# Two 3x3 convolutions on one Trainium2 core: four output columns from six terms in place of two from four

## The chip, the cores and the metric

The kernel runs on one core of one Trainium2 chip. The metric is the device time of one execution in microseconds (us), from the first to the last instruction and what lies around them; a kernel is run several times and the median is given. Engines are named as in the profile: PE is TensorE's matmul, PEld its weight load, DVE is VectorE, ACT is ScalarE, POOL is GpSimd, SP is SyncE, which here only issues transfers (DMA).

## The reference

x has 16 images of 128 channels and 32 x 32 points, all in float32. Two layers follow each other, each with a mixing part and a token part, both added to x. Layer 0 has a linear attention and a spectral filter bank (a long convolution over the 1024 tokens). Layer 1, which the change is about, is cut here to what matters:

```python
# mixing part: y = _ln_c(x), normalized over the channels
out = relu(_bn(_conv3x3(y, w1), gamma1, beta1, mean1, var1))
out = _bn(_conv3x3(out, w2), gamma2, beta2, mean2, var2)
x = x + relu(out + y)
# token part: t = _ln_t(x); 64 experts, each takes 8 tokens of an image
logits = einsum('bsd,ed->bse', t, gate_w) + gate_b
probs = softmax(logits, axis=1)                  # over the tokens
topv, topi = top_k(probs, 8)                     # by expert
# gather, weigh and sum the tokens, two linear maps with gelu, scatter back
```

The convolutions have 128 input and 128 output channels, a 3 x 3 window and a border of zeros.

## The kernel before

The program has four stretches. **Layer 0, attention** goes over the 16 samples in a period that is written out by hand (`period`): one pass issues steps of several samples, one after the other. Between them, `prepare()` prepares layer 1's weights on POOL, one step for each pass: it loads a convolution's weights (`raw`), scales them by the batch norm's factor, makes the transformed taps in `pcw`, and stores them to DRAM (`cwd`). Then it loads and scales the table of an inverse transform (`pwi`, stored as `wid`). POOL also makes the butterflies of that layer's spectra. **Layer 0, filters** (`generate` and `multiply`) follows, and ends when the spectra `ys` are stored to `yd`.

**Layer 1** is one class, `Routed`, whose methods are the steps of one sample. A function, `planned`, decides the order in which all steps of all 16 samples are issued: it takes a table that names, for each step, its engine, an assumed duration, a due time, the steps it depends on and the buffers it opens and closes, and lists the steps by a simulated start. Each engine then works through its own steps in that order, so an instruction that waits holds up everything behind it on its engine. For each sample the steps are:

- `even`, `odd`, `odd_turn`, `odd_out`, `inverse`, `add`: the inverse transform of layer 0's spectrum (L958 to L1048); PE's part is L1039, 32 instructions of 128 columns.
- `tokens` to `norm`: transposes to tokens (L149), statistics on DVE (L132), scales on POOL (L996 to L1001), normalization on ACT (L141).
- `image`, `image_copy`: transposes back (L159) and an ACT copy (L1083) into `pads`, where the image lies as two planes, of odd and of even columns, each with a border of zeros.
- The first convolution: `terms` (four DVE subtractions and additions of column planes, L920), products (L926) in two halves of the image, 16 rows each: `middle` and `outer` take two terms each. `shift` (L1097, ACT) moves the first product of `middle` out of PSUM with the batch norm's shift, `sums` (L1105, L1106) and `rows` (L1115, L1116) combine the products on DVE into the even and odd columns, and `relu` (L1119, ACT) writes them into a third pair of planes.
- The second convolution, in the same way, where `rows2` also adds the image and then relu and x (L1143, L1145).
- `tokens2` to `channels_copy`: the same normalization for the token part (copy L1158, transposes L159, copy L1179).
- For each pair of samples: logits (L1187), the choice of eight tokens (L1199 to L1220 on DVE, L1212 on ACT), and the pooled tokens (L1242, L1253).

The convolution uses the minimal scheme for two columns and three taps: four terms of four neighbouring columns, one product each with transformed taps, and two columns out of their sums. The three rows of taps (`dy`) are summed in PSUM. One product is a matmul of 128 channels by 128 channels over 256 columns, and each float32 matmul is two instructions in the profile. So one convolution of a sample has 4 terms x 3 `dy` x 2 halves = 24 matmuls, 48 instructions.

PSUM holds three sorts of tiles here: `big` (two buffers of 1024 columns), `cv` (three of 512, for the products) and `s`. In SBUF, `v` (the terms), `r` and `cs` have two buffers each.

**The experts** (`hidden`, `turn`, `output`, `collect`) go over 16 groups of four experts. Their weights are 32 blocks of 1 MB (`we`), and nine are loaded ahead into buffers that layer 1 no longer needs (`RING` names them): five once the last sample's inverse is done, four after its last `rows2`. Each further block waits until its buffer's block is used. At the end the outputs are scattered with one matmul per half (L1461), added to x and stored.

Of the kernel before, what the change touches and what calls it, by code (L numbers as in the profile page):

```python
# [57 lines left out]
HP = H + 2  # L58
WP = W // 2 + 1
HR = H // 2  # L60
WT = W // 2
# [5 lines left out]
def metaformer_kernel(ctx: ExitStack, tc: tile.TileContext, io: dict, out: bass.AP):  # L67
# [96 lines left out]
    with ExitStack() as l0:  # L164
# [7 lines left out]
        cwd = [dram.tile([P, 3, 4, C], F32, name=f"cwd{n}", tag=f"cwd{n}") for n in range(2)]  # L172
# [35 lines left out]
        with ExitStack() as a0:  # L208
# [462 lines left out]
            def prepare():  # L671
# [4 lines left out]
                for n in range(2):  # L676
                    raw = ppool.tile([P, 3, 3, C], F32, name="raw", tag="raw")
                    nc.sync.dma_start(raw.rearrange("p a b c -> p (a b) c"), io[f"w{n + 1}"])
                    cw = ppool.tile([P, 3, 4, C], F32, name="pcw", tag="pcw")
                    yield  # L680
                    scale = srow[:, n, :].unsqueeze(1).to_broadcast([P, 3, C])
                    for k in range(3):
                        eng.tensor_tensor(raw[:, :, k], raw[:, :, k], scale, ALU.mult)
                        yield
                    eng.tensor_tensor(cw[:, :, 1], raw[:, :, 0], raw[:, :, 2], ALU.add)
                    yield
                    eng.tensor_tensor(cw[:, :, 2], cw[:, :, 1], raw[:, :, 1], ALU.subtract)
                    yield
                    eng.tensor_tensor(cw[:, :, 1], cw[:, :, 1], raw[:, :, 1], ALU.add)
                    yield  # L690
                    for k, r in ((0, 0), (3, 2)):
                        nc.sync.dma_start(cwd[n][:, :, k], raw[:, :, r])
                    eng.tensor_scalar(cw[:, :, 1:3], cw[:, :, 1:3], 0.5, None, ALU.mult)
                    nc.sync.dma_start(cwd[n][:, :, 1:3], cw[:, :, 1:3])
                    yield
# [34 lines left out]
            with tc.manual_schedule(engines=PINNED):  # L730
                for p in range(-reach, B):
                    next(preparing, None)
# [117 lines left out]
    b1 = gpool.tile([E, HID], F32, name="b1")  # L850
# [4 lines left out]
    with ExitStack() as c1:  # L855
# [10 lines left out]
        RING = ("y", "z", "zt", "wi", "y", "v", "v", "cw", "pad")  # L866
        FIRST = ("wi", "v", "cw", "pad", "y")
# [23 lines left out]
        cws = first.tile([P, 2, 3, 4, C], F32, name="cw", tag="cw")  # L891
        cw = [cws[:, n] for n in range(2)]
# [8 lines left out]
        nc.sync.dma_start(b1, w1[:, C, :])  # L901


        pads = first.tile([P, 3, 2, HP, WP], F32, name="pads", tag="pad")
        nc.gpsimd.memset(pads, 0.0)

        def inner(t, hf=None):

            r0, nr = (1, H) if hf is None else (1 + hf * HR, HR)
            return bass.AP(  # L910
                t.tensor, t.offset + r0 * WP, [t.ap[0], [HP * WP + 1, 2], [WP, nr], [1, WT]]
            )

        def terms(v, p, ks):

            d = [p[:, 1 - i % 2, :, i // 2 : i // 2 + WT] for i in range(4)]
            for k in ks:
                i, j, op = ((0, 2, ALU.subtract), (1, 2, ALU.add),
                            (2, 1, ALU.subtract), (1, 3, ALU.subtract))[k]
                nc.vector.tensor_tensor(v[:, k], d[i], d[j], op)  # L920

        def products(v, wt, hf, ks):
            pc = ps.tile([P, 2, HR, WT], F32, name="pcv", tag="cv", bufs=3)
            for i, k in enumerate(ks):
                for dy in range(3):
                    nc.tensor.matmul(  # L926
                        pc[:, i], wt[:, dy, k, :], v[:, k, hf * HR + dy : hf * HR + dy + HR],
                        start=(dy == 0), stop=(dy == 2),
# [77 lines left out]
        class Routed:  # L1006


            def __init__(self, b):
                self.b = b  # L1010
                self.pr, self.j = divmod(b, 2)
                self.p1, self.p2 = pads[:, b % 2], pads[:, 2]
                self.x = xt[b]
                self.y = yts[b].rearrange("p r x e -> p (r x) e")
                self.pm, self.po, self.sd, self.r, self.ct = {}, {}, {}, {}, {}
# [66 lines left out]
            def image_copy(self):  # L1082
                nc.scalar.copy(inner(self.p1), self.px.rearrange("p (h w o) -> p o h w", w=WT, o=2))  # L1083

            def term_tile(self):
                self.v = first.tile([P, 4, HP, WT], F32, name="v", tag="v", bufs=2)

            def terms(self):
                self.term_tile()
                terms(self.v, self.p1, (1, 2, 0, 3))  # L1090

            def middle(self, hf, n=0):
                self.pm[hf] = products(self.v, cw[n], hf, (1, 2))

            def shift(self, hf, n=0):
                self.ct[hf] = work.tile([P, HR, WT], F32, name="ct", tag="ct")
                nc.scalar.activation(  # L1097
                    self.ct[hf], self.pm[hf][:, 0], AF.Identity, bias=bn[:, n, 1:2]
                )

            def sums(self, hf):

                sd = self.sd[hf] = work.tile([P, 2, HR, WT], F32, name="cs", tag="cs")
                t, pc = self.ct[hf], self.pm[hf]
                nc.vector.tensor_tensor(sd[:, 0], pc[:, 1], t, ALU.add)  # L1105
                nc.vector.scalar_tensor_tensor(sd[:, 1], pc[:, 1], -1.0, t, ALU.mult, ALU.add)  # L1106

            def outer(self, hf, n=0):
                self.po[hf] = products(self.v, cw[n], hf, (0, 3))

            def rows(self, hf):

                r = self.r[hf] = work.tile([P, 2, HR, WT], F32, name="r", tag="r")
                sd, pc = self.sd[hf], self.po[hf]
                nc.vector.tensor_tensor(r[:, 0], pc[:, 0], sd[:, 0], ALU.add)  # L1115
                nc.vector.scalar_tensor_tensor(r[:, 1], pc[:, 1], -1.0, sd[:, 1], ALU.mult, ALU.add)  # L1116

            def relu(self, hf):
                nc.scalar.activation(inner(self.p2, hf), self.r[hf], AF.Relu)  # L1119

            def terms_middle(self):
                self.term_tile()
                terms(self.v, self.p2, (1, 2))

            def terms_outer(self):
                terms(self.v, self.p2, (0, 3))

            def middle2(self, hf):
                self.middle(hf, 1)

            def shift2(self, hf):
                self.shift(hf, 1)

            def sums2(self, hf):
                self.sums(hf)

            def outer2(self, hf):
                self.outer(hf, 1)

            def rows2(self, hf):  # L1140
                self.rows(hf)
                r = self.r[hf]
                nc.vector.tensor_tensor(r, r, inner(self.p1, hf), ALU.add)  # L1143
                xh = self.x[:, hf * HALF : (hf + 1) * HALF].rearrange("p (n o) -> p o n", o=2)
                nc.vector.scalar_tensor_tensor(  # L1145
                    xh, r.rearrange("p o h w -> p o (h w)"), 0.0, xh, ALU.max, ALU.add
# [117 lines left out]
            ("even", "POOL", 1.85, -409.2, "", "z", ""),  # L1264
            ("odd", "DVE", 1.4, 60, "", "zt", ""),
            ("odd_turn", "DVE", 0.75, -162.8, "odd", "", ""),
            ("odd_out", "DVE", 1.4, 308, "odd_turn even", "", "zt"),
            ("inverse", "PE", 3.5, -181.4, "even odd_out", "big:0", "z"),
            ("add", "DVE", 1.25, 32, "inverse", "", "big:0"),
            ("tokens", "PE", 0.88, -255.4, "add", "big:1", ""),  # L1270
            ("stats", "DVE", 1.4, 65, "tokens", "", "big:1"),
            ("copy", "ACT", 1.02, -202.6, "tokens", "tok", "big:1"),
            ("variance", "POOL", 0.22, -174.5, "stats", "", ""),
            ("root", "ACT", 0.52, -164.6, "stats", "", ""),
            ("scales", "POOL", 1.75, -338.7, "variance root", "", ""),
            ("norm 0", "ACT", 0.8, -46.1, "scales copy", "", ""),
            ("norm 1", "ACT", 2.35, -0.2, "norm0", "", ""),
            ("image", "PE", 0.88, -200.9, "norm1", "big:2", "tok"),
            ("image_copy", "ACT", 1.02, -154.9, "image", "p1", "big:2"),
            ("terms", "DVE", 2.6, -242.7, "image_copy", "v:0", ""),  # L1280
            ("middle 0", "PE", 2.6, -433, "terms", "cv:0m", "v:0"),
            ("shift 0", "ACT", 0.48, -171, "middle0", "", ""),
            ("sums 0", "DVE", 0.74, -165.9, "shift0", "cs:0", "cv:0m"),
            ("outer 0", "PE", 2.6, -360.9, "terms", "cv:0o", "v:0"),
            ("rows 0", "DVE", 0.74, -387.6, "outer0 sums0", "r:0", "cv:0o cs:0"),
            ("relu 0", "ACT", 0.64, -76.6, "rows0", "p2", "r:0"),
            ("middle 1", "PE", 2.6, -189.2, "terms middle0", "cv:1m", "v:0"),
            ("shift 1", "ACT", 0.48, 17.7, "middle1", "", ""),
            ("sums 1", "DVE", 0.74, -262.2, "shift1", "cs:1", "cv:1m"),
# [311 lines left out]
```

## Time and profile before

| | us |
|---|---|
| median of three runs | 1324.69 (1323.67 to 1330.67) |
| profiled execution | 1324.0 |
| its span, first to last instruction | 1322.2 |
| layer 0, attention | 0 to 396 |
| layer 0, filters | 396 to 695 |
| layer 1: fill, run, drain | 695 to 724, 724 to 1187, 1187 to 1217 |
| experts, output | 1217 to 1293, 1293 to 1322 |

The times of the stretches count from the span's start. The mean granted clock of TensorE is 0.971 of full speed. In the profile, "L926" is line 926 of the program; a group of instructions is shown with what it writes and reads, its shape, its count, its busy time and mean duration, and the idle time of its engine just before it with what ended that. The chain of waits goes back from the last instruction to whatever released each step. An engine that is busy all the time need not be the limit, and idle time of an engine that nothing waits for costs nothing.

### The profile page before, as it was taken

How to read it: one execution, taken by the hardware profiler on the slowest of the kernel's cores; microseconds unless marked ns; L12 is line 12 of the kernel's file. 1: busy time of each engine (PE TensorE's matmuls, PEld its weight loads, DVE VectorE, ACT ScalarE, POOL GpSimd, SP SyncE). 2: the span in 40 equal slices, each digit the busy share in tenths (PEclk: the TensorE clock that was granted, in tenths of full speed). 3: DMA queues.
4: the chain of work that ended last, by engine and by line, in shares of the span. 5: the costliest groups of instructions: out<-in, count | busy, mean ns of one | idle time of the engine just before them, and what ended most of it. 6: DMA issues, size and time to landing. Idle time of an engine off the chain costs nothing. (4 is left out here: it accounts for less than half of the span.)

```text
span 1322.2 us, 33734 instructions
## 1 busy us (share of the span) xinstructions
PE 1216.7 (92%) x14116; PEld 990.8 (75%) x14116; DVE 907.2 (69%) x1982; ACT 705.2 (53%) x1424; POOL 503.3 (38%) x816
## 2 busy tenths in 40 slices
PE   4889999999998999999956999999999999996886
PEld 3777777777767888888846987989888888883443
DVE  5688887877765666776637767777778676772224
ACT  3777777777545666666623435545555454544111
POOL 2324545454685777777743111222212121110002
PEclk8899999999998999999987999999999999997998
DMA  7014343433344333333367211313122113007986
GB/s 268 17 35 140 118 134 112 144 124 121 114 149 145 127 125 127 127 121 119 107 235 182 70 48 49 88 27 111 32 80 64 33 49 127 17 24 260 374 329 255
DMA packets 87401, 162.99 MB, mean 123 GB/s; under 512 B 5584, under 2 KB 40784, under 8 KB 86864
## 3 DMA queue, kind: packets, MB, share of 16 engines
q1 hardware_dynamic: 86608, 158.33, 36.2%
q8 instruction: 111, 1.82, 0.6%
q0 software_dynamic: 640, 2.49, 0.5%
q14 instruction: 42, 0.34, 0.1%
HBM read 104.18 MB, written 56.62 MB: 122 GB/s over the span
## 5 line engine op out<-in xcount | busy, mean ns | idle before, releaser
L926 PE MATMUL pcv<-v,cw 128*128 128x256 f32 x1536 | 342.9, 380 | 0.0
L926 PEld LDWEIGHTS pcv<-v,cw 128*128 128x128 f32 x1536 | 286.8, 190 | 42.2 <-issue 5.7
L785 ACT COPY g<-pg 128x512 f32<-128x512 f32 x288 | 153.1, 591 | 102.8 <-PE pg L776 102.8
L783 DVE COPY g<-pg 128x512 f32<-128x512 f32 x224 | 145.8, 687 | 90.1 <-PE pg L776 90.1
L776 PE MATMUL pg<-ph,mst 32*128 32x128 f32 x4096 | 155.3, 287 | 4.5 <-ACT g L785 3.0
L776 PEld LDWEIGHTS pg<-ph,mst 32*128 32x128 f32 x4096 | 130.7, 190 | 30.8 <-issue 25.9
L796 PE MATMUL py<-g,v 128*32 128x128 f32 x4096 | 140.1, 276 | 3.8 <-POOL v L768 1.2
L796 PEld LDWEIGHTS py<-g,v 128*32 128x32 f32 x4096 | 105.3, 110 | 20.7 <-issue 2.4
L767 POOL TENSOR_TENSOR v<-xc 128x256 f32<-128x256 f32 x128 | 91.6, 741 | 71.6 <-PE py L796 62.5
L141 ACT ACTIVATE tok<-tok,sts 128x128 f32<-128x128 f32 x256 | 101.8, 481 | 23.8 <-POOL sts L1001 20.4
L132 DVE BATCH_NORM_STATS2 bst<-big 128x6 f32<-128x256 f32 x256 | 91.1, 417 | 19.5 <-PE big L154 12.1
L1066 POOL TENSOR_SCALAR sts<-bst 128x8 f32<-128x8 f32 x16 | 6.5, 406 | 235.7 <-DVE bst L132 235.7
L920 DVE TENSOR_TENSOR v<-pads 128x544 f32<-128x544 f32 x128 | 85.0, 723 | 9.9 <-ACT pads L1119 9.5
L618 PE MATMUL big<-u,mu 128*128 128x128 f32 (+4 forms) x384 | 86.0, 380 | 0.0
L274 POOL TENSOR_TENSOR xf<-ab 128x256 f32<-128x256 f32 x34 | 24.8, 730 | 132.0 <-DVE ab L241 131.9
L618 PEld LDWEIGHTS big<-u,mu 128*128 128x128 f32 x384 | 56.7, 191 | 18.0 <-issue 15.4
L1097 ACT ACTIVATE ct<-pcv,bn 128x256 f32<-128x256 f32 x64 | 30.3, 474 | 68.8 <-PE pcv L926 67.9
L551 PE MATMUL big<-wf,ub 128*128 128x256 f32 x256 | 62.0, 385 | 0.2
L149 PEld LDWEIGHTS big<-ident,x 128*128 128x128 f32 x384 | 47.3, 148 | 19.2 <-issue 7.2
L149 PE MATMUL big<-ident,x 128*128 128x128 f32 x384 | 53.6, 286 | 8.5 <-DVE x L1048 3.4
L1115 DVE TENSOR_TENSOR r<-pcv,cs 128x256 f32<-128x256 f32 x64 | 26.9, 420 | 49.0 <-PE pcv L926 48.2
L141 ACT ACTIVATE tt<-tt,sts 128x128 f32<-128x128 f32 x128 | 51.1, 480 | 9.2 <-POOL sts L1001 8.9
(231 smaller groups left out, 2271.3 us busy)
## 6 DMA issues: line engine op xcount, KB each, us to landing
we<-in_weight SPq DMA_DIRECT2D x32, 1024.0 KB, 9.7
vd<-xf SPq DMA_DIRECT2D x16, 1024.0 KB, 5.1
xc<-vd SPq DMA_DIRECT2D x64, 256.0 KB, 3.5
yd<-ys SPq DMA_DIRECT2D x32, 512.0 KB, 3.8
y<-yd SPq DMA_DIRECT2D x15, 896.0 KB, 6.5
x<-in_x SPq DMA_DIRECT2D x16, 512.0 KB, 4.1
mi<-in_M_phi SPq DMA_DIRECT2D x16, 512.0 KB, 4.9
xd<-x SPq DMA_DIRECT2D x16, 512.0 KB, 6.0
```

The costliest lines, as they stand in the source:

```text
L132: nc.vector.bn_stats(bst[:, j : j + 2, :].rearrange("p j s -> p (j s)"), src[:, j : j + 2, :].rearrange("p j c -> p c j"),)
L141: nc.scalar.activation(dst[:, j, :], src[:, j, :], AF.Identity, bias=nm[:, j : j + 1], scale=r[:, j : j + 1],)
L149: nc.tensor.transpose(pt[:, j, :], src[:, j * P : (j + 1) * P], ident)
L551: nc.tensor.matmul(dst, self.ub[:, q, :], wf[:, q, :], start=True, stop=True)
L618: nc.tensor.matmul(self.pa[:, a:hi], mu[:, NF - 1 - si, tap, :], self.u[:, a - tap : hi - tap], start=(tap == 0), stop=(tap == KU - 1),)
L767: nc.gpsimd.tensor_tensor(vv[:, x, 1:, bs], e, o, op)
L776: nc.tensor.matmul(pg[r][:, i], mst[rs, 4 * q + i, :], ph[rs, c, :], start=True, stop=True,)
L783: nc.vector.tensor_copy(dst, src)
L785: nc.scalar.copy(dst, src)
L796: nc.tensor.matmul(py[rows, x, kl, :], v[:, (x * NM + m) * JL + jl, 1 - ri : 3 - ri, :] .rearrange("p k b -> p (k b)"), g[:, ((x * 2 + ri) ...
L920: nc.vector.tensor_tensor(v[:, k], d[i], d[j], op)
L926: nc.tensor.matmul(pc[:, i], wt[:, dy, k, :], v[:, k, hf * HR + dy : hf * HR + dy + HR], start=(dy == 0), stop=(dy == 2),)
```

## The change

Both convolutions now use the scheme for **four** columns and three taps: six terms of six neighbouring columns, six products, four columns from their sums. The image lies as four planes of 32 x 8 columns, so that one product covers the whole image with 256 columns. The rows of taps above and below leave out the row that would fall on the border (248 columns). One convolution has 6 terms x 3 `dy` = 18 matmuls, 36 instructions.

- The **first convolution's terms** come from PE: the normalized tokens are multiplied by a constant matrix `bt` (128 x 192) that holds the six terms of four image rows, eight matmuls a sample into two `big` tiles, which ACT copies to `va`. They no longer read the image, which is now used for the addition alone.
- The **second convolution's terms** are made by DVE from planes with rows of nine, of which one column is zero (`padded`); the six terms are computed without gaps over 288 columns, and the products read eight of each nine.
- The sums are new: `inside_sums`, `columns`, `edges`, and `rest` for the second convolution. The batch norm's shift moves into `relu` (as its bias) and into `rest`.
- `va`, `vb` and `r` have one buffer each.
- `prepare` makes six transformed taps in place of four, and takes two steps for each of the later passes in place of one.
- Layer 1's table has new steps, durations and due times, and `planned` now takes a tile's buffers strictly in turn.
- Smaller moves: `b1` is loaded late in layer 1 into `tok`'s buffer, in place of before layer 1; `RING` is reordered (still nine); `ot`, `ht` and some later loads use other buffers.

```diff
                 for p in range(-reach, B):
-                    next(preparing, None)
+                    for _ in range(2 if p >= -2 else 1):
+                        next(preparing, None)
...
-        RING = ("y", "z", "zt", "wi", "y", "v", "v", "cw", "pad")
+        RING = ("y", "z", "wi", "y", "cw0", "v", "cw1", "zt", "pad")
...
-        pads = first.tile([P, 3, 2, HP, WP], F32, name="pads", tag="pad")
-        nc.gpsimd.memset(pads, 0.0)
+        pads = first.tile([P, 2 * N + 4 * PLANE], F32, name="pads", tag="pad")
...
+        nc.gpsimd.memset(pads[:, 2 * N :], 0.0)
...
-        def products(v, wt, hf, ks):
-            pc = ps.tile([P, 2, HR, WT], F32, name="pcv", tag="cv", bufs=3)
+        def products(v, wt, ks):
+            pc = ps.tile([P, 2, IMG], F32, name="pcv", tag="cv", bufs=3)
             for i, k in enumerate(ks):
-                for dy in range(3):
+                for dy in (1, 0, 2):
+                    lo, hi = max(0, 1 - dy), min(H, H + 1 - dy)
                     nc.tensor.matmul(
-                        pc[:, i], wt[:, dy, k, :], v[:, k, hf * HR + dy : hf * HR + dy + HR],
-                        start=(dy == 0), stop=(dy == 2),
+                        pc[:, i, lo * GT : hi * GT], wt[:, dy, k, :],
+                        v[:, k, lo + dy - 1 : hi + dy - 1],
+                        start=(dy == 1), stop=(dy == 2),
                     )
...
+            def terms(self, i):
+                pv = self.pv[i] = big().rearrange("p (j w) -> p j w", j=4)
+                for j in range(4):
+                    nc.tensor.matmul(
+                        pv[:, j, : NTERM * 4 * GT], self.tok[:, 4 * i + j], bt, start=True, stop=True
+                    )
...
+            def inside_terms(self):
+                v = self.v = vb
+                zt = self.zt = work.tile([P, 4, PLANE], F32, name="zt", tag="zt", bufs=1)
+                nc.vector.scalar_tensor_tensor(
+                    zt[:, 0:2], columns(2, 1), -4.0, columns(4, 3), ALU.mult, ALU.add
+                )
+                nc.vector.tensor_tensor(v[:, 1], zt[:, 0], zt[:, 1], ALU.add)
+                nc.vector.tensor_tensor(v[:, 2], zt[:, 0], zt[:, 1], ALU.subtract)
...
+            def product(self, n, ks):
+                v = va if n == 0 else vb.rearrange("p t (h k) -> p t h k", k=ROW)[..., :GT]
+                self.pc[ks] = products(v, cw[n], ks)
...
+            def columns(self):
+                nd = work.tile([P, 2, IMG], F32, name="zt", tag="zt", bufs=1)
+                m = self.pc[3, 4][:, 0]
+                nc.vector.scalar_tensor_tensor(nd[:, 0], self.ctn, 0.5, m, ALU.mult, ALU.add)
+                nc.vector.scalar_tensor_tensor(nd[:, 1], m, 2.0, self.ctn, ALU.mult, ALU.subtract)
+                r = self.r = work.tile([P, 4, IMG], F32, name="r", tag="r", bufs=1)
+                nc.vector.tensor_tensor(r[:, 0:2], nd, self.sd, ALU.add)
+                nc.vector.scalar_tensor_tensor(r[:, 2:4], nd, 4.0, self.sd, ALU.mult, ALU.add)
...
+            def rest(self):
+                self.edges()
+                r = self.r
                 nc.vector.scalar_tensor_tensor(
-                    xh, r.rearrange("p o h w -> p o (h w)"), 0.0, xh, ALU.max, ALU.add
+                    r, r, bn[:, 1, 1:2], self.p1.rearrange("p o h k -> p o (h k)"), ALU.add, ALU.add
+                )
+                xs = self.x.rearrange("p (n o) -> p n o", o=4)
+                nc.vector.scalar_tensor_tensor(
+                    xs, r.rearrange("p o n -> p n o"), 0.0, xs, ALU.max, ALU.add
                 )
```

## The prediction

> **What bounds the kernel now.** I read the page first: busy shares, then the 40 slices.
>
> ```profile
> PE 1216.7 (92%) x14116; PEld 990.8 (75%) x14116; DVE 907.2 (69%) x1982; ACT 705.2 (53%) x1424; POOL 503.3 (38%) x816
> ...
> PE   4889999999998999999956999999999999996886
> ```
>
> 92% is a mean over stages. The change sits in layer 1, so the second view is the table of stretches, cut where the chain of waits and the timeline show layer 1 filling (to 724), running (to 1187) and draining (to 1217); the columns are length, then busy time of PE, PEld, DVE, ACT, POOL with instruction counts, granted clock, DMA.
>
> ```profile
> 695.00:724.00 29.00, 19.27 (x122) 17.47 (x123) 22.95 (x51) 8.48 (x19) 9.85 (x21) 0.77 0.66 168
> 724.00:1187.00 463.00, 461.24 (x2717) 404.64 (x2716) 350.35 (x755) 232.10 (x468) 90.55 (x226) 1.00 0.20 59
> 1187.00:1217.00 30.00, 17.81 (x117) 11.98 (x115) 9.83 (x19) 15.18 (x27) 2.18 (x11) 0.77 0.67 245
> ...
> 860.00:981.00 121.00, 121.00 (x739) 106.40 (x737) 94.56 (x207) 63.52 (x128) 25.77 (x64) 1.00 0.22 61
> ```
>
> Between 860 and 981, PE is busy all the time at full clock. Since a busy PE need not be PE at its peak, I went to the chain of waits, merged in order of time (start, length, what):
>
> ```profile
> 856.33 2.59 PE pcv L926 x12
> 859.80 10.36 PE pcv L926 x48
> 870.16 1.75 PE big L159 x16
> ...
> 917.01 2.59 PE pcv L926 x12
> 920.48 10.36 PE pcv L926 x48
> 930.84 1.75 PE big L159 x16
> ```
>
> The same pieces come back after 920.48 - 859.80 = 60.68 us: one pair of samples, **30.34 us a sample**, and the chain is matmuls without a gap. So in this stretch time is the number of matmul instructions times their spacing: 2.59/12 = 0.216 us for one of 256 columns (each f32 matmul is two instructions). From the same chain: inverse 3.57/32 = 0.112 us for 128 columns, 8 transposes 0.87 us. Check: 96 x 0.216 + 3.57 + 4 x 0.87 + half of a pair's logits 1.87, turn 0.87, pool 1.90 and last transpose 0.11 = 30.2.
>
> The groups in 860 to 981 say what the other engines have left (busy, mean ns, idle before it and its releaser):
>
> ```profile
> L920 DVE TENSOR_TENSOR v<-pads 128x544 f32<-128x544 f32 x32 | 21.5, 729 | 1.5 <-ACT pads L1119 1.5
> L1115 DVE TENSOR_TENSOR r<-pcv,cs 128x256 f32<-128x256 f32 x16 | 6.7, 421 | 12.6 <-PE pcv L926 12.4
> L1105 DVE TENSOR_TENSOR cs<-pcv,ct 128x256 f32<-128x256 f32 x16 | 6.7, 417 | 5.8 <-ACT ct L1097 5.8
> ```
>
> DVE is busy 94.56/121 x 30.34 = 23.7 us a sample and idle 6.6, mostly waiting for PE. ACT has 15.9.
>
> **The change, part by part**, against the profiled execution: 1324.0 us (span 1322.2 and 1.8 around it), 0.7 below the median 1324.69.
>
> **Convolutions on PE.** Before: per convolution 4 terms x 3 rows of taps x 2 halves = 24 matmuls, 48 instructions. After: 6 terms x 3 rows = 18 matmuls, 36 instructions; 12 have 256 columns, and 24 (dy 0 and 2 leave out one row of 8) have 248. Between 0.112 us at 128 and 0.216 at 256 columns the line gives 0.209 at 248 and 0.164 at 192. One convolution: 12 x 0.216 + 24 x 0.209 = 7.61 us, was 48 x 0.216 = 10.37. Two convolutions, 16 samples: 32 x 2.76 = 88.3 us gone.
>
> **First terms on PE.** 8 matmuls of 192 columns = 16 instructions x 0.164 = 2.62 us a sample, 41.9 in all. Their weights (PEld 190 ns each) lie under matmuls as those of the inverse do (192 ns each, spacing 112). Net on PE: 88.3 - 41.9 = **-46.4**, 2.9 a sample: a period of 27.4 if PE stays gapless. It counts fully, since these matmuls are the chain.
>
> **Rows of nine.** The second convolution's moving operand now comes in runs of eight words with one skipped; before it was contiguous. No row shows this. Matmuls of L618 start one word off (tap 1) at the same spacing, which says 0. Weight loads of L154, with a hop before every word, take 189 ns where L159's contiguous ones take 141:
>
> ```profile
> L154 PEld LDWEIGHTS big<-ident,x x128: 185/189/209, 69.9 to 374.6; 128*128 128x128 f32 x128
> ...
> L159 PEld LDWEIGHTS big<-ident,tok x256: 137/141/230, 29.5 to 1137.1; 128*128 128x128 f32 x128
> ```
>
> That is 0.38 ns a hop. With 32 hops an instruction, 36 instructions, 16 samples: +7. I take +1, nearer to L618, which is also a moving operand; a gain is excluded, as the columns are the same.
>
> **DVE.** From the rows, one column costs 1.04 ns and an instruction some 0.15 us on top, of which 0.08 hides behind an independent one. First convolution: sums 0.75, columns 2.1, edges 0.69. Second terms: 1.57 + 1.57 + 1.5. Second convolution: sums 0.75, columns 2.1, rest 0.69 + 1.25 + 1.28. Sum 14.25 us. Removed: 8 terms 5.25, four pairs of sums and four of rows 6.0, rows2's tail 2.84, sum 14.1. So DVE stays at 23.8, but its idle share shrinks from 6.6 to 3.6 us. It is in order: behind a columns instruction waiting for ACT's copy lie the next statistics, odd sums and terms, and PE waits for those. Bounds of the stalls: 0 (PE runs two samples in turn) and 1 us a sample, 16. I take 0.25 a sample, +4, since DVE's waits now are for PE, not the reverse.
>
> One DVE row is disputed. The last instruction of rest reads r with a hop of 256 words before every element. L1145 reads and writes x two words apart and takes 693 ns for 512, as contiguous L1143 (692); L1048 reads PSUM 128 words apart at 1222 ns for 1024. By these it costs nothing, and the 1.28 stands.
> The Trainium skill, Vector Engine (DVE) Microarchitecture Reference, section Measured stream behaviour on trn2, speaks against it: one source hopping at every element takes 1.73 ns a column against 1.05; by that, rest would be 0.7 us longer and DVE's idle time 2.9 us a sample, which leaves the sum as it is while PE sets the period.
>
> **ACT.** Goes: four shifts 1.9. Comes: two copies of 768 (between 0.59 at 512 and 1.01 at 1024: 0.80 each), four of 256 (0.37 to 0.47). About +1.4, 17.3 of 27.4 us: hidden by PE; without that cover, 16 x 1.4 = 22.
>
> **Setting up the weights (layer 0).** By the rows of L685 (1.0 us for 384 columns) and L693 (2.15 for 768), POOL gets 2 x (5 instructions of about 1.05, one of 2.15 and one more of 1.0) = +16.8 us, in periods of some 20 us in which it is busy 155.88 of 302 us. Two steps now go in one period. Once a weight load (pwi) and its first use meet in the same period, and POOL waits some 5 us (that load's time to landing), with that period's butterflies behind it. SP issues two more stores and each load still precedes x loads needed two periods later. Bounds 0 and 5; POOL's idle half hides most: +1.
>
> **Start of layer 1.** cw grows from 2 x 768 to 2 x 1152 KB, bt adds 96, b1's 128 moves to the end: +736 KB on SP's queue ahead of y and x. At the 331 GB/s of 677 to 685 that is 2.3 us, beside the last products, before the store of 684.7 that the chain follows. Bounds 0 and 4: +1. The memset of pads shrinks from 3468 to 1152 words (2.99 us to about 1.0), and DVE's ys waited 2.4 for it: -1 (0 to -2). Terms no longer wait for the image, but PE fills that gap with inverses now too: 0.
>
> **Drain.** After the last product, rest (3.2) precedes the tokens; before, rows 0.75 and 1.4 (1187.6 to 1189.8): +1. And with whole images rather than halves, the last sample's way from edges over relu (2 x 0.62) to its first terms (1.57), some 3.5 us, may lie open: +2. Bounds 0 and 6: +3. Prefetched halves stay nine, b1's new place and gates 4 wait for nothing late: 0.
>
> **Sum:** -46.4 + 1 + 4 + 1 + 1 - 1 + 3 = -37.4; 1324.0 - 37.4 = **1287**.
>
> **The rivals.**
> 1. *Hand-overs eat part.* va, vb and r have one buffer each, and big's two serve two more users a sample, so copy, sums, columns, edges, relu and terms follow each other in turn. For: DVE's idle time nearly halves. Against: PE has no gap now. At 0.7 to 2 us a sample: -46.4 + 11 to 32 and the other +5, 1294 to 1315. Chance 0.20.
> 2. *PE's work does not shrink.* If the 16 loads of the first terms (190 ns) did not lie under their matmuls, these cost up to 0.354 us each, 16 x 16 x 0.19 = 49 more: 1324.0 - 37.4 + 49 = 1336 at most, half of it 1311; taken at three quarters, 1324. Against: the inverse's loads. Chance 0.07.
> 3. *Slower: DVE sets the period.* Waits at columns (for ACT's copy and PE's second pair) put DVE in turn with PE rather than beside it. DVE's 23.8 us and 6.6 idle give 30.4, no gain; from an idle of 6.6 us a sample on it is slower. At 8: 31.8, (31.8 - 30.34) x 16 = +23 and the other +5: 1352. The granted clock would add to it: it was 0.77 where PE was busy two thirds (695 to 724). Against: DVE's waits in the groups are for PE. Chance 0.10.
> The Trainium skill, TensorE: Matmul & The Clock Gate, Part 1, has the clock halve after an idle window of about 3.4 us; the row shows lower clocks only at the stage's ends, and by that rule gaps below the window cost their own length alone.
>
> **How the numbers follow.** Forecast (1274 to 1300) 0.63, rivals 0.20, 0.07, 0.10. The range, 1274 to 1312: below by the bounds of gap rows, stalls, memset and drain (-46.4 - 2 - 1), above it takes in most of rival 1 and the sum with half of all upper bounds. Leaving out rival 3, rival 2's most and rival 1's end leaves 0.18 out. A measurement of this kernel tells some 0.5%, 6.6 us, from no change: faster 0.63 + 0.18 = 0.81, same 0.08 (rival 2, rival 1's end), slower 0.11.
>
> **What would show it.** Right: a repeat of about 55 us a pair in the chain of waits, PE's groups there without idle time, 36 instructions a convolution in 7.6 us, the terms at 0.164 each. Wrong: second convolution's spacing above the first's (rows of nine); idle time of PE released by DVE or ACT in the middle (rivals 1, 3); rest's last instruction well above 1.28 us (its hops).

## The result, and the profile after

No change: **1324.74 us** (median of 20 runs, 1319.44 to 1330.4) against 1324.87 (20 runs, 1317.39 to 1331.94), ratio **1.0008, interval 0.9993 to 1.0023**. The forecast was 1287, the range 1274 to 1312. The profiled execution's span is 1320.6 us, 1.6 less than before.

First the page of the changed kernel, its line of engines and PE's 40 slices:

```profile
PE 1180.8 (89%) x13988; PEld 958.8 (73%) x13988; DVE 928.2 (70%) x1918; ACT 722.8 (55%) x1456; POOL 507.7 (38%) x830
...
PE   4889999999988999999947989999999999866875
```

128 instructions fewer, as worked out, and 35.9 us less busy time; the span did not follow. PE's share fell from 92% to 89%: work became idle time. Where, the table of stretches tells, cut at the same piece of the chain in each kernel (four pairs of samples in the steady state; length, busy PE, PEld, DVE, ACT, POOL, clock, DMA). Before, then after:

```profile
859.80:1102.50 242.70, 242.70 (x1477) 213.44 (x1477) 187.72 (x407) 127.39 (x256) 50.13 (x126) 1.00 0.19 56
```

```profile
861.80:1095.50 233.70, 224.72 (x1412) 197.80 (x1412) 201.01 (x381) 135.63 (x273) 47.33 (x128) 1.00 0.20 57
```

Before, PE had no gap; after, it is idle 9.0 of 233.7 us at full clock, so about 2.2 us a pair. DVE is idle as well (32.7 us), so neither engine is busy all the time there. The chain of waits of the changed kernel (start, length, what) shows one such gap:

```profile
861.82 5.34 PE pcv L948 x24
...
871.48 0.69 DVE r L1175
872.17 1.33 DVE bst L131 x4
...
873.69 0.71 DVE zt L1127
...
877.03 0.68 DVE v L1143
...
877.73 0.77 DVE v L1146
...
878.54 5.34 PE pcv L948 x24
...
907.75 0.77 DVE v L1143
...
908.54 0.77 DVE v L1146
...
909.36 2.80 PE pcv L948 x12
...
920.25 4.92 PE pcv L948 x22
```

A pair now takes 920.25 - 861.82 = **58.43 us** (60.68 before), and twice in it the path leaves PE and goes through DVE: the 24 instructions at 878.54 and the 12 at 909.36 start 0.04 to 0.05 us after L1146 ends (and the 12 take 2.80 us behind the gap, 2.54 elsewhere). The waits between 730 and 1180 (who, for what, us in total, times, longest) put a sum to it, and the page's groups (busy, mean ns, idle before it) agree:

```profile
PEld pcv L948 <- DVE v L1146: 25.9, 16, 2.6
PE pcv L948 <- DVE v L1146: 20.6, 16, 2.3
...
DVE v L1143 <- PE pcv L948: 9.4, 10, 3.5
```

```profile
L948 PE MATMUL pcv<-v,cw 128*128 128x248 f32 (+1 forms) x1152 | 262.5, 381 | 23.9 <-DVE v L1146 20.6
```

L1146 is the second instruction of `outer_terms`, which the diff above does not show:

```python
def outer_terms(self):
    v05 = self.v[:, 0::5]            # planes 0 and 5 of six
    nc.vector.scalar_tensor_tensor(v05, columns(0, 1), 4.0, columns(4, 5), ALU.mult, ALU.add)      # L1143
    nc.vector.scalar_tensor_tensor(v05, columns(2, 3), -5.0, v05, ALU.mult, ALU.add)               # L1146
```

It writes planes 0 and 5. The 24 instructions at 878.54 are `inside_b` and `next_b`, which read planes 1 to 4, ready since L1131 and L1137; the 12 at 909.36 are the next sample's `next_b`, which reads planes 3 and 4. They need nothing of L1146 and yet wait for it. And where `inside_b` is issued first, L1143 waits for *it* (9.4 us in all), as if it overwrote what `inside_b` reads.

### The profile page after: what moved, and what is told of

Same layout as the page of the kernel before. It is cut to its first block, busy times and chain, and to the rows that moved or that the text cites. A ratio compares the mean times of both kernels' runs of the same rounds, so it can differ in the third digit from the quotient of the medians.

```text
span 1320.6 us, 33472 instructions
## 1 busy us (share of the span) xinstructions
PE 1180.8 (89%) x13988; PEld 958.8 (73%) x13988; DVE 928.2 (70%) x1918; ACT 722.8 (55%) x1456; POOL 507.7 (38%) x830
## 5 line engine op out<-in xcount | busy, mean ns | idle before, releaser
L948 PE MATMUL pcv<-v,cw 128*128 128x248 f32 (+1 forms) x1152 | 262.5, 381 | 23.9 <-DVE v L1146 20.6
L948 PEld LDWEIGHTS pcv<-v,cw 128*128 128x128 f32 x1152 | 215.0, 191 | 56.0 <-DVE v L1146 25.9
L140 ACT ACTIVATE tok<-tok,sts 128x128 f32<-128x128 f32 x256 | 101.9, 481 | 32.8 <-POOL sts L1024 29.5
L131 DVE BATCH_NORM_STATS2 bst<-big 128x6 f32<-128x256 f32 x256 | 91.1, 417 | 35.9 <-ACT tt L1257 19.8
L273 POOL TENSOR_TENSOR xf<-ab 128x256 f32<-128x256 f32 x34 | 24.8, 729 | 115.7 <-DVE ab L240 115.6
L1156 ACT ACTIVATE ct<-pcv 128x256 f32<-128x256 f32 x64 | 24.2, 378 | 73.7 <-PE pcv L948 73.7
L1062 PE MATMUL big<-wi,z 128*128 128x128 f32 x384 | 51.9, 288 | 6.2 <-DVE z L1008 3.4
```

The lines of the kernel that those rows point to most:

```text
L131: nc.vector.bn_stats(bst[:, j : j + 2, :].rearrange("p j s -> p (j s)"), src[:, j : j + 2, :].rearrange("p j c -> p c j"),)
L140: nc.scalar.activation(dst[:, j, :], src[:, j, :], AF.Identity, bias=nm[:, j : j + 1], scale=r[:, j : j + 1],)
L948: nc.tensor.matmul(pc[:, i, lo * GT : hi * GT], wt[:, dy, k, :], v[:, k, lo + dy - 1 : hi + dy - 1], start=(dy == 1), stop=(dy == 2),)
L1062: nc.tensor.matmul(self.px[:, q * P : (q + 1) * P], zq, wi[:, q, r, :], start=(r == 0), stop=(r == 1),)
```

## The experiments

Theory A: the program orders a stepped write by the whole range it spans, planes 0 to 5, so that products of planes 1 to 4 and this write wait for each other. Theory B: DVE has become the limit, by `rest`'s hopping read (L1244) above all.

Each ratio below is to the kernel before, run beside the experiment, with its 95% interval in brackets; the changed kernel itself stands at 1.0008.

**1. The two planes side by side.** The planes of `vb` are stored in the order 1, 2, 3, 4, 0, 5. Every engine issues the same instructions in the same order; only L1143 and L1146 now write one block.

```diff
-                v05 = self.v[:, 0::5]
+                v05 = self.v[:, 4:6]
...
-                self.pc[ks] = products(v, cw[n], ks)
+                self.pc[ks] = products(v, cw[n], ks, ((0, 1, 2, 3, 4, 5), (4, 0, 1, 2, 3, 5))[n])
```

> The kernel after, with the second convolution's terms stored in the order 1, 2, 3, 4, 0, 5, so that outer_terms writes one contiguous piece and not every fifth plane. Same instructions in the same order. Theory A (the write to planes 0 and 5 is ordered against planes 1 to 4 between them, so that the inside and next products wait for outer_terms, and outer_terms for the products): PE's waits for L1146, 20.6 us between 730 and 1180, go to about 0 but for the outer products, and a pair takes 55.5 to 57 us in place of 58.4; 12 to 24 us less. Theory B (DVE's load of 25.1 us a sample paces): PE waits for the next DVE step instead, a pair stays at 58, under 4 us less. Theory C (single buffers of va, vb and r pace): the same as B.

Measured: **1292.43 us** (1291.07 to 1295.79), ratio 0.9781 [0.9747, 0.9815]. The chain of waits, and the stretch that answers to those above:

```profile
849.62 5.34 PE pcv L948 x24
...
892.34 5.08 PE pcv L948 x24
...
905.51 1.54 PE pcv L948 x6
```

```profile
849.60:1073.20 223.60, 221.76 (x1414) 197.83 (x1413) 200.08 (x381) 134.72 (x273) 48.57 (x128) 1.00 0.21 60
```

A pair takes 55.89 us, PE's idle time falls from 9.0 to 1.8 us, and L1146 is gone from PE's waits (of DVE's, 2.9 us for L1130 are left). Between the first two of these pieces the chain runs through ACT and POOL for 14 us (862.18 to 876.50), in which PE is idle for only 0.44 us. Theory A holds, with the same work on every engine. The time fell by more than the 12 to 24 us that were expected: of 26.6 us between the profiled spans, 24.6 lie in the run, and 3.4 in layer 0, which the edit does not touch.

**2. `rest` without the hop.** The last instruction reads r in its stored order, so other points are added to x.

```diff
-                    xs, r.rearrange("p o n -> p n o"), 0.0, xs, ALU.max, ALU.add
+                    xs, r.rearrange("p o n -> p (o n)").rearrange("p (n o) -> p n o", o=4), 0.0, xs, ALU.max, ALU.add
```

> The kernel after, but rest's last instruction reads r in its stored order, without the hop of 256 words before each element; this adds other points of r to x than the reference asks. The instruction should take 1.28 us in place of 1.97. Theory A: it lies beside PE's work in the run, so 0 to 4 us less in all. Theory B: DVE has 0.7 us a sample less, 16 x 0.7 = 11 us less.

Measured: 1319.0, ratio 0.9974 [0.9957, 0.9992]. The instruction in the changed kernel, and here (busy, mean ns):

```profile
L1244 DVE SCALAR_TENSOR_TENSOR x<-r,x 128x1024 f32<-128x1024 f32 x4 | 7.9, 1972 | 0.1
```

```profile
L1244 DVE SCALAR_TENSOR_TENSOR x<-r,x 128x1024 f32<-128x1024 f32 x4 | 4.9, 1224 | 0.1
```

The hop costs 0.75 us a sample, 12 us of DVE's time in all, of which some 3 us reach the end (1 to 6 by the interval). The loss is not here.

**3. Both edits.**

> Both edits: terms stored in the order 1, 2, 3, 4, 0, 5, and rest's last instruction reading r in its stored order (other points of r are added to x than the reference asks). Theory A: as the first alone, and up to 5 us more. Theory B: as the second alone, 11 us less than after. If both limit in turn, the sum of both, 20 to 35 us less.

Measured: 1298.96 (1291.36 to 1299.72), 0.9814 [0.9772, 0.9855]; a pair takes 55.89 us, no less than in experiment 1, and by their intervals the two times cannot be told apart. With the false wait gone, the hop is off the path.

**4. Experiment 1 with `rest`'s last instruction cut to 64 of 1024 columns**, which leaves nearly all of that addition out.

```diff
-                    xs, r.rearrange("p o n -> p n o"), 0.0, xs, ALU.max, ALU.add
+                    self.x[:, 0:64], r[:, 0, 0:64], 0.0, self.x[:, 0:64], ALU.max, ALU.add
```

> Terms stored in the order 1, 2, 3, 4, 0, 5, and rest's last instruction cut to 64 columns, so that almost all of the second convolution's result is not added to x: DVE has 1.8 us a sample less to do, 23.3 of 27.4. Theory A: PE has no gaps left either way, the pair is at 55 to 56 us and the time within 6 us of the first kernel's. Theory B: 16 x 1.8 = 29 us less than the first kernel's, until PE has no gaps.

Measured: 1300.04, 0.9838 [0.9797, 0.9879]; a pair takes 55.85 us. DVE has over 1.7 us less to do in each sample, and the period stays. Theory B falls. The time is 7.6 us longer than in experiment 1, just beyond the 6 us that theory A allowed; in the profiled execution the experts' stage, which began at half clock, is alone 5.7 us longer (last section).

**5. The changed kernel's layout, but one plane an instruction.** Experiment 1 moved data too; this one does not.

```diff
-                v05 = self.v[:, 0::5]
...
+                for i, k in enumerate((0, 5)):
+                    v = self.v[:, k]
...
```

> The changed kernel with its own layout of planes, but the outermost terms are written one plane at a time: four DVE instructions of 288 columns where there were two of 576 that step over the planes between (some 0.2 to 0.3 us more DVE work a sample). Theory A (the stepped write counts as a write to the planes between, so the inner products wait for it): the wait of PE for the outermost terms goes, a pair takes about 56 us, and the time is near that of the kernel with the two planes side by side, 1290 to 1300 us, ratio about 0.98. Rival (what helped was where the planes lie, or DVE's load): a pair stays at 58.4 us and the time at 1320 to 1325 us, or a little more by the added DVE work.

Measured: 1306.05 (1300.89 to 1307.67), 0.9841 [0.9808, 0.9874]. A pair takes 910.39 - 854.05 = 56.34 us, and no wait of PE for the outermost terms is left: it was the one instruction that spans the planes, not where they lie. The time missed its forecast by 6 us. Of the 11.9 us by which the profiled span is longer than experiment 1's, 5.2 lie in the experts, which began at half clock, 2.9 in layer 0, which the edit does not touch, and 2.4 in the run, where the four instructions take 0.59 us more DVE time a sample than the two (two of 450 and two of 598 ns for 749 and 758).

**6. The drain.** Experiment 1, and for the last sample `stats2` is issued before `copy2`.

> The kernel with the two planes side by side, and for the last sample alone the statistics are issued before the copy of the same PSUM tile. Theory (DVE's statistics wait for ACT's copy of the same tile, 1.0 us, on the open path after the last product): the stretch from the last product to the last store of layer 1 falls from 34.6 us to some 33.5 us and the time by 1 us at most. Rival (that path is not what ends last there): the stretch stays at 34.6 us. The steady state is the same by both, a pair 55.9 us.

Measured: 1296.25 (1290.13 to 1298.88), 0.9767 [0.973, 0.9803]; the drain is 33.7 us for 34.6, as the theory said, but not for its reason. The statistics now start 0.1 us behind the tokens, yet the copy (1.01 us) then stands ahead of ACT's root in ACT's order: from the tokens' end to the channels it takes 5.39 us for 5.49, a gain of 0.1. What shortened the drain is the logits, 3.72 us for 4.85, by where the half clock fell. In the kernel before, the copy comes behind the root, beside POOL's scales, and the same stretch takes 4.43 us; that order was not tried here. The whole time cannot be told from experiment 1's.

The copy and the statistics of the last sample in experiment 1, and here (start, length, what, idle before it):

```profile
1156.78 1.01 ACT L1257 COPY tt<-big 128x1024 f32<-128x1024 f32 x1 [3.25 <-PE big L148]
1157.89 1.43 DVE L131 BATCH_NORM_STATS2 bst<-big 128x6 f32<-128x256 f32 x4 [2.30 <-ACT tt L1257]
```

```profile
1155.39 1.43 DVE L131 BATCH_NORM_STATS2 bst<-big 128x6 f32<-128x256 f32 x4 [1.25 <-PE big L148]
...
1156.90 1.01 ACT L1257 COPY tt<-big 128x1024 f32<-128x1024 f32 x1 [4.85 <-DVE bst L131]
```

**7. The planner told.** The false wait stays, and the table names it.

```diff
-            ("inside_b", "PE", 2.55, 19.6, "inside_terms", "cv:b12", "vb:b"),
-            ("next_b", "PE", 2.55, -209.2, "next_terms", "cv:b34", "vb:b"),
+            ("inside_b", "PE", 2.55, 19.6, "outer_terms", "cv:b12", "vb:b"),
+            ("next_b", "PE", 2.55, -209.2, "outer_terms", "cv:b34", "vb:b"),
```

> The changed kernel with its stepped write kept, but the planner's table says that the inner products of the second convolution follow outer_terms, as they do in fact; the planner makes another order of it. Theory A1 (the loss is that the planned order does not know of the wait): the new order hides most of it, a pair takes 56 to 57 us, time 1295 to 1308 us. Theory A2 (the wait itself costs, whatever the order: DVE's seven steps between relu and the outermost terms lie open): a pair stays at 58 us or more, 1318 to 1328 us.

Measured: **1376.63**, ratio 1.0379 [1.0335, 1.0424]: slower by 50 us, which neither theory had. Its chain of waits:

```profile
862.39 0.77 DVE zt L1127
...
867.19 0.77 DVE v L1146
...
868.00 7.03 PE pcv L948 x24
...
898.13 0.68 DVE zt L1127
...
901.90 0.77 DVE v L1146
...
902.71 5.34 PE pcv L948 x24
```

In this order all of DVE's seven steps lie on the path in every sample (5.6 and 4.6 us), and a pair takes 967.38 - 902.71 = 64.67 us. The clock adds to it: before the first 24 instructions PE is idle for 3.61 us, and they take 7.03 us for 5.34, at a mean granted clock of 0.57 from 868 to 872; the same comes again in the next pair. So A1 fell, and A2 has only its direction: an order that is true to the wait can be worse than one that ignores it. Whether another order would hide the wait was not tried.

**8. The kernel before once more**, beside experiment 9.

> The kernel before itself, unchanged, for a second profile of it beside the next run on one chip. The stage of the experts took 75.6 us there and 78.1 to 78.7 us in the changed kernels whose clock was full at its start, with weights arriving at 402 against 382 GB/s. Theory (the difference belongs to the kernels: other buffers, other order of arrival): it comes again, some 75.6 us and 400 GB/s here, and 78 us or more beside it. Rival (it belongs to the chip and execution): both show the same.

Measured: 1325.36 us in one run; its experts take 77.6 us, with the weights at 404 GB/s. Beside it on the chip, experiment 9 has 79.8 us and 387. The rate goes with the kernel: 402 and 404 in the kernel before, 382 to 387 in the changed ones whose clock is full there. The stage's time does less so: the 75.6 us did not come again, and the kernel before differs by 2.0 us from itself, as much as the 2.2 between the two here. Why the changed kernels' loads are slower is open.

**9. The clock in the drain.** Experiment 1 with products of the identity that nobody reads, in PE's gaps.

```diff
+                if b == B - 1 and name in ("tokens2", "channels", "turn"):
+                    pd = ps.tile([P, 512], F32, name="pd", tag="cv", bufs=3)
+                    for _ in range({"tokens2": 12, "channels": 20, "turn": 32}[name]):
+                        nc.tensor.matmul(pd[:, 0:P], ident, ident, start=True, stop=True)
```

> The kernel with the two planes side by side, and in the drain of layer 1 TensorE gets 64 f32 products of the identity that nobody reads (12 before the last tokens, 20 before the last channels, 32 before the last turn; 0.22 us each, in gaps of 3.2, 5.5 and 8.1 us). Theory (the granted clock falls to 0.5 to 0.6 while TensorE waits there, and its 56 matmuls of the drain take 13.4 us for 5.5 at full clock): the clock stays near 1, the drain falls from 34.6 to 27 to 30 us, the experts' stage stays at 78 us in every execution, and the time is 1284 to 1288 us with less scatter. Rival (the clock there is lowered by something else, or the fillers hold up the real matmuls): the drain stays at 34 us or grows, 1292 to 1300 us.

Measured: 1293.58 (1291.09 to 1297.17), 0.9775 [0.9723, 0.9828], the same as experiment 1. The drain falls by 2.3 us to 32.3, the experts take 1.1 more. The expected 27 to 30 us missed: PE's timeline (start, length, what, idle before it) shows the last turn and the pooling at full speed (1.07 and 1.97 us for 1.94 and 3.33 in experiment 1, together the 2.2 us that were won), the logits still at half. The channels, 3.17 us for 3.18, had nothing to win: each waits for ACT's normalization of its tile.

```profile
1164.14 4.84 PE L1286 MATMUL big<-tk,gw 128*64 128x512 f32 x8
1168.91 7.62 PE L1453 MATMUL pd<-ident 128*128 128x128 f32 x64
1177.03 1.07 PE L148 MATMUL big<-ident,gt 128*128 128x128 f32 x8 [0.50 <-DVE gt L1319]
```

## Why the prediction was wrong

By stages, in us of the profiled executions (layer 0 to the first inverse; from there to the first product; first to last product; to the first expert's product; to the first product of the output; the rest):

| | layer 0 | fill | run | drain | experts | end | span |
|---|---|---|---|---|---|---|---|
| before | 694.8 | 28.9 | 463.5 | 30.3 | 75.6 | 29.1 | 1322.2 |
| after | 693.3 | 24.8 | 460.7 | 33.7 | 78.4 | 29.7 | 1320.6 |
| experiment 1 | 689.9 | 25.2 | 436.1 | 34.6 | 78.7 | 29.5 | 1294.0 |

**The step that failed is the stall term**, "I take 0.25 a sample, +4", with its bounds 0 and 16, and with it "PE runs two samples in turn". Its spacing sum gives a period of 30.34 - 2.76 x 2 + 2.62 = 27.44 us; measured are 58.43/2 = 29.2, so the stalls are 1.8 us a sample, 28 in all, beyond the upper bound of 16. The run shows what stood in its place: not DVE's load (experiment 4) but a wait that the change adds and that I did not see in `0::5`. Taking it away gives 24.6 us of the run back (460.7 to 436.1), and leaves stalls of 0.5 us a sample, 8 in all, within the bounds. The prediction had looked only for waits of one step for another's result or for its buffer; this one is between steps that share no data.

Point by point:

- **PE's sum, -46.4: right.** 12 product instructions take 2.54 us where 2.53 was worked out, and eight instructions of the first terms, half a sample's, 1.30 us, 0.163 each for 0.164; their weight loads lie under them. Rival 2 is out; that its case "taken at three quarters" stood at 1324, the time that was measured, is chance.
- **Rows of nine, +1: nothing.** 12 product instructions take 2.54 us in both convolutions.
- **Rivals 1 and 3: the size of rival 1's loss, not its reason.** It said that hand-overs by single buffers would eat 11 to 32 us, for 1294 to 1315 in all. The stalls of 28 us lie in the first range and the time beyond the second; and the single buffers stay in experiment 1, where a pair takes 55.89 us, 0.5 us a sample above the sum. DVE does not set the period (experiment 4), though it is busy 25.1 us a sample for the 23.8 forecast; 0.7 of the 1.3 is the hop.
- **`rest`'s hop: wrong row.** I took 1.28 us by L1145 and L1048; it is 1.97. The Trainium skill, Vector Engine (DVE) Microarchitecture Reference, section Measured stream behaviour on trn2, has 1.73 ns a column for one source that hops 4 KiB at every element (here the hop is 1 KiB), by estimate 1.8 us for 1024 columns and some 1.9 with what an instruction costs on top: the page was nearer than my rows. PE's path hides most of it, as the prediction said.
- **Start of layer 1, 0 in sum:** the fill is 4.1 us shorter. **Drain, +3:** measured +3.4, in part by luck: the tokens start 1.8 us later behind the last product where +1 was forecast, and 1.05 more go to ACT's copy ahead of the statistics (5.48 us from the tokens' end to the channels for 4.43), which no term had; the +2 was for a place ahead of the last product. **Weights of layer 0, +1:** layer 0 ends 1.5 us earlier. **Prefetch, 0:** the experts take 2.8 us longer than in the first profile of the kernel before, 0.8 longer than in the second (experiment 8), loads being the last waits there.
- **Against experiment 1**, which has the change without the false wait, the sum of -37.4 still promised 9 us more than the -28.2 of the spans. The drain with +4.3, the experts with +3.1, and 4.5 us in which PE is idle in the last 78 us of the run (none before) are larger than forecast; the remaining difference has parts of both signs and is not assigned.

## What to carry to other kernels

A new write that steps over parts of a tile is a wait to be looked for: follow each slice that a step writes to every reader within its span, not only to the readers of its data. If a released engine does not make the whole faster, look in the chain of waits for a hand-over between two steps that share nothing; storing what is written together side by side costs no instruction and gave 2.2% here. Naming the wait in the planner's table did not mend it here: that cost 4%, taking the wait away gained 2%.

## What the hardware showed that was not expected

**Half the clock without a long gap.** In experiment 9 the longest stretch in which PE was idle in the 10 us up to 1162 is 1.01 us. Eight transposes follow it one by one, each behind ACT's normalization, 3.17 us for what takes 0.87 in a row. The granted clock stood at 0.50 from 1162.6 to 1169.2, and the logits took 4.79 us there and 1.87 in the steady state. Two slices of that execution (length, busy PE, PEld, DVE, ACT, POOL, clock, DMA):

```profile
1150.00:1161.00 11.00, 9.49 (x82) 9.03 (x80) 5.62 (x8) 3.04 (x6) 1.44 (x7) 1.00 0.89 312
1161.00:1171.00 10.00, 9.73 (x32) 4.63 (x33) 0.83 (x1) 4.81 (x9) 0.00 (x0) 0.66 0.68 245
```

The Trainium skill, TensorE: Matmul & The Clock Gate, Part 1, has the clock halve after an idle window of about 3.4 us. That does not fit this row, where no stretch of 3.4 us was idle. Two other places do fit: 3.61 us of idle in experiment 7 brought the half clock, and in the changed kernel's steady state 1.64 us of idle in every pair left it at 1.00 (861.8 to 1095.5). So a short gap between full work was harmless here, and a shorter one followed by thin work was not; that it is the thin work which counts is argued from this one place. The products that nobody reads do hold the clock: it is 1.00 from 1171 to 1182.3, where experiment 1 has 0.63 (1172 to 1186).

**The drain's low clock can reach into the next stage.** In experiments 4, 5 and 6 the profiled execution's first 13 to 14 us of experts ran at 0.50, and that stage took 83.9 to 84.4 us; at 1.00, as after the change and in experiments 1 and 3, 78.0 to 78.7. The first 8 us of that stage in experiment 1 and in experiment 5:

```profile
1186.00:1194.00 8.00, 7.21 (x84) 2.21 (x76) 0.98 (x2) 1.20 (x2) 0.00 (x0) 1.00 0.99 370
```

```profile
1192.00:1200.00 8.00, 7.84 (x34) 1.19 (x35) 0.11 (x1) 0.84 (x2) 0.00 (x0) 0.50 0.81 280
```

In experiment 4 PE is busy for 8.00 of the 8 us up to 1191.2 at 0.50, and the clock is back only some 6 us later: being busy for 8 us did not bring it back. That this is also what scatters the times of one kernel by some 5 us is likely. The mean clock of each execution fits: the 13 of the kernel before beside experiments 1 to 4 go from 1318.43 us at 0.972 to 1328.16 at 0.966. Where in the execution the clock was lost, those without a profile do not show.
